# A graph layer on one core: degrees from first edges, degree products in four portions, statistics ahead of comparisons, wider scatter fills

## The chip, the cores and the metric

One Trainium2 chip, one of its cores. The metric is the device time of one execution in microseconds. The core's engines work side by side, each through its own queue in order: TensorE (PE in the profile, its weight loads apart as PEld), VectorE (DVE), ScalarE (ACT), GpSimd (POOL) and SyncE (SP), whose queue here only issues transfers. POOL also issues the indexed transfers (gathers and scatters).

## The reference

A layer norm in front, a message-passing layer over four relations, and a feed-forward block, on 625 nodes of 512 features and 20,625 edges sorted by destination (10,000 in both directions, and a loop per node). Cut to what matters:

```python
h = relu(layernorm(x))
for r in range(4):
    w_r = where(edge_type == r, edge_weight, 0)
    total_msg += (h[src] @ W_rel[r] + b_rel[r]) * w_r[:, None]
agg = segment_sum(total_msg, dst, 625)
deg = segment_sum(edge_weight, dst, 625)
agg = agg / maximum(deg, 1)[:, None]
hh = h @ W_self + b_self + agg
x1 = layernorm(h + hh) * ln1_g + ln1_b
ffn = gelu(x1 @ W_ffn1 + b_ffn1) @ W_ffn2 + b_ffn2
out = x + layernorm(x1 + ffn) * ln2_g + ln2_b
```

The change is about `deg`, the weighted degree of each node, and about the order of the work that stands beside it.

## The kernel before

Nodes lie in five blocks of 128 (`NB`), edges in 162 tiles of 128 (`NT`). The kernel first makes a **table** in device memory: for every relation and block, `table_rows` multiplies the transposed block `hT[i]` with the relation's weights (four pairs of matrix instructions, so eight by the profile's count), VectorE evicts the product (L358) and SP stores it. These are 20 steps, `step = r * NB + i`. In relation 0, `next_transposed` (L957) turns the next block in the middle of a step's products: `transposed` needs `z[:, i + 1]`, which `x_stats` (bn_stats, L335) and `pre_norm` (L325, and a root on POOL, L302) make on VectorE.

The first manual schedule (L937 to L998) writes down the order of TensorE, VectorE, ScalarE and POOL by hand: per engine, the instructions stand as the lines are called. A second one (L1273) emits a planned order for everything after the table; some of its first VectorE operations (L515, L525) appear in the trace among the last ones of the first schedule.

Besides the table, that first loop does four other jobs:

- **Block 0's sums.** Each edge of block 0's 31 columns of edges (`LN`) is compared with its 63 neighbours on either side (`line_sums`, L603 to L611, in `pieces` of four, eight, eight, eight and three columns, at the steps of `COLUMNS_AT`). POOL then scatters each column's weights into `cells` (`scatter`, L617), followed by a fill of the tile `idle` that only keeps POOL busy. At most `PACE * (step + 1)` scatters are issued up to a step. `load_sums` (L628) reads `cells` back as `sums_w`, which TensorE needs in the first product after the table (L1166).
- **Edge columns** at step 5: destination, relation and row numbers as columns (`outer_columns`, `edge_columns`, `degree_columns`, `group_columns`).
- **Degrees.** Node by node, a degree is a product of a 0/1 matrix with weights. `degree_hots` compares each tile's destinations with a window of 38 node rows (`W`), in bf16, 27 tiles to a chunk (`DG`). `degree_sums` multiplies, per tile, `w3` (the weight in three bf16 parts, and a 1) with that matrix into the two accumulators `pdeg`: three rows add up to the degree, the fourth counts edges per node. All six chunks are multiplied at step 13; `degree_end` and `spread_rows` bring the sums into columns, `rdeg` becomes the reciprocal.
- **First edges.** In the inner blocks three consecutive edges form a group (`EG`; 30 groups of tiles from tile 35 on, `GROUPS`, `GROUP0`): tile q of a group holds every group's edge q. Edges 1 and 2 of a group count for the group's sum only where they have the first one's destination (`wgt_g`). Where a node's edges begin inside a group, `first_edges` works out the group's number (`x_group`) from the counts, `load_first_edges` gathers it (`x_edges`), and `first_columns` (called by the later plan) makes columns and weights (`x_on`) of those edges.

`count_outside` counts edges outside their windows; were there any, a slow path would do all again.

Of the kernel before, what the change touches and what calls it, by code (L numbers as in the profile page):

```python
# [16 lines left out]
P = 128  # L17
# [120 lines left out]
def gnn_layer(ctx, tc, x, edges, edge_line, edge_groups, w_self, w_rel, w_ffn1, w_ffn2, rows_in, bf1_in, out, n_edges):  # L138
# [92 lines left out]
    load_x(3, 4)  # L231
    nc.sync.dma_start(cells[:P * NC * P, :].rearrange("(p c n) o -> p c (n o)", p=P, n=D // 2),
                      zeros.bitcast(F32).unsqueeze(1).to_broadcast([P, 2 * NC * P // D, D // 2]))
    load_x(4, NB)
# [35 lines left out]
    x_found = const.tile([P, 1], F32, name="x_found")  # L270
    wgt_g = const.tile([P, GROUPS, EG - 1], F32, name="wgt_g")
# [342 lines left out]
    idle = const.tile([P, PAUSE], BF16, name="idle")  # L614
# [25 lines left out]

    def degree_columns():
        nc.vector.tensor_sub(lim[:, 2, :], dst_f, starts.rearrange("p a b -> p (a b)")[:, :NT])
        nc.vector.tensor_sub(lim[:, 2, :], lim[:, 2, :], shift[:, 1, :])
        rel = early.tile([P, NT], BF16, name="rel")
        nc.vector.tensor_copy(rel, lim[:, 2, :])
        row_w = const.tile([P, W], BF16, name="row_w")
        nc.vector.tensor_copy(row_w, node_row[:, :W])
        w3 = const.tile([P, NT, 4], BF16, name="w3")
        nc.vector.memset(w3, 1.0)
        rest = lim[:, 3, :]  # L650
        nc.vector.tensor_copy(w3[:, :, 0], wgt)
        nc.vector.tensor_sub(rest, wgt, w3[:, :, 0])
        nc.vector.tensor_copy(w3[:, :, 1], rest)
        nc.vector.tensor_sub(w3[:, :, 2], rest, w3[:, :, 1])
        nc.vector.tensor_scalar(node_i[:, 1, :], node_i[:, 1, :], P - 1, None, op0=ALU.bitwise_and)
        nc.vector.tensor_copy(dst_mod, node_i[:, 1, :])
        return rel, row_w, w3
# [23 lines left out]
    def degree_sums(j0, nj, oc, w3):  # L681

        for j in range(j0, j0 + nj):
            s = ep.starts[j]
            lo, hi = max(s, 0), min(s + W, NP)
            for q in range(lo // D, (hi - 1) // D + 1):
                a, z_ = max(lo, q * D), min(hi, (q + 1) * D)
                if q not in pdeg:
                    pool, tag = (ps_add, "add") if q == 0 else (ps, "ps")
                    pdeg[q] = pool.tile([P, D], F32, tag=tag, name=f"pdeg_{q}")  # L690
                    nc.tensor.matmul(pdeg[q][:4, :], zeros[:, :4], zeros, start=True, stop=False)
                last = j == NT - 1 or ep.starts[j + 1] >= (q + 1) * D
                nc.tensor.matmul(pdeg[q][:4, a - q * D:z_ - q * D], w3[:, j, :], oc[:, j - j0, a - s:z_ - s],  # L693
                                 start=False, stop=last)
# [5 lines left out]
    def first_edges():  # L700
# [18 lines left out]
    def first_columns():  # L719
# [13 lines left out]
        nc.vector.tensor_mul(x_on, x_on, x_edges[:, :, 1:, 3].bitcast(F32))  # L733
        nc.vector.tensor_mul(x_on, x_on, rdeg[:, 1:NB - 1].unsqueeze(2).to_broadcast([P, INNER, EG - 1]))

    def degree_end():
# [5 lines left out]
        def spread_rows():  # L742
# [10 lines left out]
            nc.vector.tensor_scalar(rdeg, rdeg, 1.0, None, op0=ALU.max)  # L753
            nc.vector.reciprocal(rdeg, rdeg)
# [149 lines left out]
    DG = 27  # L904
# [22 lines left out]
    chunks = [(j0, min(DG, NT - j0)) for j0 in range(0, NT, DG)]  # L927
# [9 lines left out]
    with tc.manual_schedule(engines={PE, DVE, ACT, mybir.EngineType.Pool}):  # L937
# [6 lines left out]
        stats = x_stats(1)  # L944
        hots, made = [], 0
# [53 lines left out]
        assert not columns and not pieces and made == len(chunks) and len(scattered) == LN  # L999
# [405 lines left out]
```

## Time and profile before

| | us |
|---|---|
| median of three runs | 281.29 |
| the three runs | 282.1, 281.29, 280.1 |
| the profiled execution | 281.09 |
| its span, first to last instruction | 279.3 |
| busy: TensorE, VectorE, ScalarE, POOL | 253.7, 198.2, 82.1, 196.5 |
| first gather of table rows | 91.98 |

A timeline row reads: start and duration in us, engine, line, operation, what it writes and from what, shape, count of instructions merged, and in brackets the engine's idle time before it and what ended that. A row of the chain of waits has start, duration, engine and line. A row of stretches has the stretch, its length, busy time (and count) of PE, PEld, DVE, ACT and POOL, the granted TensorE clock as a share of full speed, the DMA engines' share, and GB/s. A row of groups has the total, the mean in ns, and the idle time before its instructions.

### The profile page before, as it was taken

What the parts mean: (1) busy time and instruction counts of PE and PEld (TensorE: products, weight loads), DVE (VectorE), ACT (ScalarE), POOL (GpSimd) and SP (SyncE); (2) the same over time, 40 slices, a digit from 0 to 9 for tenths busy, and PEclk for the clock granted to TensorE, in tenths of its full rate; (3) what the DMA queues carried; (4) which work ended last, traced back from release to release, by engine and by line L of the source; (5) the groups of instructions that cost most, each with busy time, mean ns of one, the idle gap of its engine ahead of it and who ended that gap; (6) DMA issues with size and microseconds to landing.
All of it is one profiled execution on the core that took longest, in us unless ns stands there. A gap on an engine that the chain in (4) does not pass through costs nothing.

```text
span 279.3 us, 3679 instructions
## 1 busy us (share of the span) xinstructions
PE 253.7 (91%) x1081; PEld 141.5 (51%) x1081; DVE 198.2 (71%) x469; ACT 82.1 (29%) x190; POOL 196.5 (70%) x378
## 2 busy tenths in 40 slices
PE   8897999999999998876798969999999999998990
PEld 3433444465544443533354424459476783853960
DVE  4985799983559641898978768658669986856514
ACT  3110030000000385683946022224234252430320
POOL 6788998997030788887887878888889888831000
PEclk9999999999999999999689999999999999999997
DMA  7999899631722888988665796766666668640001
GB/s 218 380 424 394 229 372 346 217 116 38 263 80 89 299 257 282 332 263 313 181 185 169 253 323 213 235 188 188 189 186 182 186 171 255 190 133 13 38 2 39
DMA packets 25127, 58.86 MB, mean 211 GB/s; under 512 B 3937, under 2 KB 6241, under 8 KB 24850
## 3 DMA queue, kind: packets, MB, share of 16 engines
q0 software_dynamic: 9488, 27.57, 32.9%
q1 hardware_dynamic: 15328, 29.60, 29.9%
q10 hardware_dynamic: 290, 1.44, 1.5%
q8 instruction: 9, 0.15, 0.2%
q14 instruction: 12, 0.10, 0.1%
HBM read 50.75 MB, written 7.85 MB: 210 GB/s over the span
## 4 chain that ended last, share of the span: by engine, by line
PE 47%; DVE 16%; POOL 16%; DMA 11%; issue 7%; ACT 1%; DVEq 0%; SPq 0%; POOLq 0%
PE pt L351 19%; POOL ms L1033 11%; DMA ms<-table,row_i 9%; PE pu L830 7%; PE po L848 5%; PE acc L1166 4%; PE acc L1083 4%; POOL zeros L1036 3%; PE pz L371 3%; DVE ea L1061 2%; PE pdeg L693 2%; DMA xs<-in_x_dram 1%; DVE od L525 1%; PE bank L548 1%; DVE es L1061 1%
## 5 line engine op out<-in xcount | busy, mean ns | idle before, releaser
L1033 POOL DMA_INDIRECT ms<-table,row_i x99 | 98.3, 993 | 32.0 <-DVE x_cols L724 12.3
L351 PE MATMUL pt<-wr,hT 128*128 128x512 f32 x160 | 70.4, 595 | 0.2 <-DMA wr<-in_L_gnn_W_rel_dram 0.2
L351 PEld LDWEIGHTS pt<-wr,hT 128*128 128x128 f32 x160 | 29.8, 190 | 35.0 <-issue 34.6
L617 POOL DMA_INDIRECT cells<-weight,cell x31 | 37.1, 1197 | 6.1 <-issue 5.0
L1061 DVE SCALAR_TENSOR_TENSOR ea<-ms,wgt_g,ea 128x512 f32<-128x512 f32 x40 | 30.0, 750 | 15.2 <-DMA ms<-table,row_i 13.3
L830 PEld LDWEIGHTS pu<-x1T,w_sb 128*128 128x128 f32 x320 | 37.5, 192 | 5.7 <-issue 3.8
L533 ACT ACTIVATE ohw<-os,w 128x128 fp32r<-128x128 f32 x64 | 20.1, 389 | 63.8 <-DVE os L515 63.6
L830 PE MATMUL pu<-x1T,w_sb 128*128 128x128 f32 (+1 forms) x320 | 38.0, 275 | 0.9 <-ACT x1T L1215 0.9
L1043 ACT ACTIVATE ea<-ms,ed 128x512 f32<-128x512 f32 x30 | 20.7, 691 | 59.6 <-DMA ms<-table,row_i 46.6
L848 PE MATMUL po<-w_sb,gT 128*128 128x512 f32 (+3 forms) x96 | 36.0, 522 | 0.0
L1083 PE MATMUL acc<-es,oh 128*128 128x512 f32 x58 | 30.7, 619 | 1.8 <-DVE rs_z L766 0.9
L1036 POOL MEMSET zeros<- 128x200 bf16 x99 | 28.8, 290 | 0.0
L1166 PE MATMUL acc<-tr,sums_w 128*128 128x512 f32 x60 | 27.5, 592 | 0.0
L358 DVE SCALAR_TENSOR_TENSOR m<-pt,rx,brel_bc 128x512 f32<-128x512 f32 x20 | 14.8, 745 | 13.8 <-PE pt L351 13.8
L848 PEld LDWEIGHTS po<-w_sb,gT 128*128 128x128 f32 (+1 forms) x96 | 16.6, 188 | 14.8 <-issue 12.3
L548 PE MATMUL bank<-od,ohw 128*128 128x500 f32 (+16 forms) x64 | 17.1, 393 | 4.9 <-ACT ohw L533 4.1
L371 PE MATMUL pz<-ws_sb,hT 128*128 128x512 f32 x40 | 19.6, 612 | 0.8 <-DVE n_out L419 0.8
L1061 DVE SCALAR_TENSOR_TENSOR es<-ms,wgt_g,ea 128x512 f32<-128x512 f32 x20 | 14.8, 742 | 6.8 <-DMA ms<-table,row_i 6.6
L834 ACT ACTIVATE gT<-pu,bf 128x128 f32<-128x128 f32 (+1 forms) x40 | 13.7, 364 | 16.5 <-PE pu L830 16.4
L548 PEld LDWEIGHTS bank<-od,ohw 128*128 128x128 f32 x64 | 11.2, 202 | 12.5 <-ACT ohw L533 6.7
L1166 PEld LDWEIGHTS acc<-tr,sums_w 128*128 128x128 f32 x60 | 11.2, 190 | 12.4 <-issue 12.4
L1083 PEld LDWEIGHTS acc<-es,oh 128*128 128x128 f32 x58 | 10.3, 194 | 12.7 <-issue 5.3
(191 smaller groups left out, 289.4 us busy)
## 6 DMA issues: line engine op xcount, KB each, us to landing
tr<-table SPq DMA_DIRECT2D x14, 512.0 KB, 5.8
table<-m SPq DMA_DIRECT2D x20, 256.0 KB, 2.2
w_sb<-in_L_gnn_W_ffn_dram SPq DMA_DIRECT2D x2, 2048.0 KB, 12.7
wr<-in_L_gnn_W_rel_dram SPq DMA_DIRECT2D x3, 1024.0 KB, 8.1
ms<-table,row_i POOLq DMA_INDIRECT x99, 3.7
rows<-in_rows_dram SPq DMA_DIRECT2D x1, 1536.0 KB, 13.0
cells<-zeros SPq DMA_DIRECT2D x1, 1280.0 KB, 9.5
sums_w<-cells ACTq DMA_DIRECT2D x1, 1280.0 KB, 6.4
```

The costliest lines, as they stand in the source:

```text
L351: nc.tensor.matmul(p, hT[i][:, k, :], wr_sb[r][:, k, :], start=(k == 0), stop=(k == KD - 1))
L371: nc.tensor.matmul(p[0], hT[i][:, k, :], ws_sb[:, k, :], start=(k == 0), stop=(k == KD - 1))
L548: nc.tensor.matmul(bank[b, n0][:, (lo - n0) * NC:(end - n0) * NC], box["ohw"][:, k - k0, part, :], box[k][:, :(end - lo) * NC], start=star ...
L617: i = nc.gpsimd.indirect_dma_start(out=cells[:, :], out_offset=bass.IndirectOffsetOnAxis(ap=cell[:, k:k + 1], axis=0), in_=weight[:, k:k + ...
L830: nc.tensor.matmul(pu[:, :nn], w1_sb[:, k, f * P:(f + 1) * P], x1T_b()[:, k, :nn], start=(k == 0), stop=(k == KD - 1))
L848: nc.tensor.matmul(po[h][:n, :w], box["gT"][:, f, at], w2_sb[:, f, c], start=(f == 0), stop=(f == KF - 1))
L1033: nc.gpsimd.indirect_dma_start(out=ms[j], out_offset=None, in_=table[:, :], in_offset=bass.IndirectOffsetOnAxis(ap=row_i[:, j:j + 1], axis=0))
L1036: nc.gpsimd.memset(zeros[:, :PAUSE], 0.0)
L1043: nc.scalar.activation(box["sum"], ms[j], AF.Copy, scale=wgt[:, j:j + 1])
L1061: nc.vector.scalar_tensor_tensor(to, ms[j], wgt_g[:, k, q - 1:q], box["sum"], op0=ALU.mult, op1=ALU.add)
L1083: nc.tensor.matmul(acc[bs], ohs[0][:, q, :].bitcast(F32), box["sum"], start=(k == 0), stop=last)
L1166: nc.tensor.matmul(acc[b,], sums_w[b][:, c, :], kept[(b, c) if (b, c) in kept else c], start=first, stop=last)
```

## The change

Degrees: of each group of three tiles only the first stays in the degree product, with the weight of the whole group as far as the destinations agree (`wgt_g` summed, plus the first's weight). The 1 that counts stands only at first edges of groups, so the counts give the group's number without a division. What a node has in the group where it begins inside is added later, in `first_columns`, where clamp and reciprocal of `rdeg` now stand too. 102 tiles are left (`ND`), in four chunks of up to 26.

Order: a chunk is compared at steps 7, 8, 10 and 11 (`HOTS_AT`) and multiplied right after the next step's table products; the degrees' later steps come one step earlier. Group and degree columns move from step 5 to step 6, group first. `x_stats` and `pre_norm` of block `step + 3` stand ahead of the comparisons of edge columns, which move to steps 0, 2, 4, 9 and 12. Block 1's `pre_norm` is called ahead of `set_limits` (72 small fills on POOL). The count of outside edges comes one step earlier, `load_sums` one step later. Blocks 3 and 4 of x are loaded in one transfer ahead of the zero fill of `cells`. The fill after a scatter has 400 elements in place of 200, and the pace is 3.

```diff
-    load_x(3, 4)
+    load_x(3, NB)
     nc.sync.dma_start(cells[:P * NC * P, :].rearrange("(p c n) o -> p c (n o)", p=P, n=D // 2),
                       zeros.bitcast(F32).unsqueeze(1).to_broadcast([P, 2 * NC * P // D, D // 2]))
-    load_x(4, NB)
...
-    idle = const.tile([P, PAUSE], BF16, name="idle")
+    idle = const.tile([P, 2 * PAUSE], BF16, name="idle")
...
+    deg_tiles = [*range(GROUP0), *range(GROUP0, GROUP0 + EG * GROUPS, EG), *range(GROUP0 + EG * GROUPS, NT)]
+    ND = len(deg_tiles)
+    deg_at = [(slice(0, GROUP0), slice(0, GROUP0)), (slice(GROUP0, GROUP0 + GROUPS), None),
+              (slice(GROUP0 + GROUPS, ND), slice(GROUP0 + EG * GROUPS, NT))]
...
-        rel = early.tile([P, NT], BF16, name="rel")
-        nc.vector.tensor_copy(rel, lim[:, 2, :])
+        rel = early.tile([P, ND], BF16, name="rel")
...
-        w3 = const.tile([P, NT, 4], BF16, name="w3")
-        nc.vector.memset(w3, 1.0)
-        rest = lim[:, 3, :]
-        nc.vector.tensor_copy(w3[:, :, 0], wgt)
-        nc.vector.tensor_sub(rest, wgt, w3[:, :, 0])
+        w3 = const.tile([P, ND, 4], BF16, name="w3")
+        nc.vector.memset(w3, 0.0)
+        nc.vector.memset(w3[:, deg_at[1][0], 3], 1.0)
+        whole, rest = early.tile([P, ND], F32, name="deg_w"), lim[:, 3, :ND]
+        for to, of in deg_at:
+            if of is None:
+                nc.vector.tensor_copy(rel[:, to], grouped(lim[:, 2, :])[:, :, 0])
+                nc.vector.reduce_sum(whole[:, to], wgt_g, axis=mybir.AxisListType.X)
+                nc.vector.tensor_add(whole[:, to], whole[:, to], grouped(wgt)[:, :, 0])
+            else:
+                nc.vector.tensor_copy(rel[:, to], lim[:, 2, of])
+                nc.vector.tensor_copy(whole[:, to], wgt[:, of])
+        nc.vector.tensor_copy(w3[:, :, 0], whole)
+        nc.vector.tensor_sub(rest, whole, w3[:, :, 0])
...
-                    pool, tag = (ps_add, "add") if q == 0 else (ps, "ps")
-                    pdeg[q] = pool.tile([P, D], F32, tag=tag, name=f"pdeg_{q}")
+                    pdeg[q] = ps_add.tile([P, D], F32, tag="add", name=f"pdeg_{q}")
...
-        near = 1.5 * 2.0 ** 23
-        g = xw[:, 1, :]
-        nc.vector.tensor_scalar(g, first[:, :INNER], -(GROUP0 * P + (EG - 1) / 2), 1.0 / EG, op0=ALU.add, op1=ALU.mult)
-        nc.vector.tensor_scalar(g, g, near, None, op0=ALU.add)
-        nc.vector.tensor_scalar(g, g, -near, 0.0, op0=ALU.add, op1=ALU.max)
-        nc.vector.tensor_scalar(x_group, g, float(GROUPS * P), None, op0=ALU.min)
+        nc.vector.tensor_scalar(x_group, first[:, :INNER], -1.0, 0.0, op0=ALU.add, op1=ALU.max)
...
+        nc.vector.reduce_sum(x_deg, x_on, axis=mybir.AxisListType.X)
+        nc.vector.tensor_add(rdeg[:, 1:NB - 1], rdeg[:, 1:NB - 1], x_deg)
+        nc.vector.tensor_scalar(rdeg, rdeg, 1.0, None, op0=ALU.max)
+        nc.vector.reciprocal(rdeg, rdeg)
         nc.vector.tensor_mul(x_on, x_on, rdeg[:, 1:NB - 1].unsqueeze(2).to_broadcast([P, INNER, EG - 1]))
...
-    DG = 27
+    DG = 26
-    PACE = 2
+    PACE = 3
-    COLUMNS_AT = 0, 1, 4, 7, 10
-    COLUMNS_OF_EDGES_AT, LOAD_AT = 5, 16
-    DEGREES_AT, SPREAD_AT, FIRST_AT = 13, 14, 15
+    COLUMNS_AT, HOTS_AT = (0, 2, 4, 9, 12), (7, 8, 10, 11)
+    COLUMNS_OF_EDGES_AT, LOAD_AT = 5, 17
+    DEGREES_AT, SPREAD_AT, FIRST_AT = 12, 13, 14
...
-        stats = x_stats(1)
+        pre_norm(1, x_stats(1))
...
-        pre_norm(1, stats)
         line_columns()
-        stats = x_stats(2)
+        pre_norm(2, x_stats(2))
...
                     transposed(hT[i + 1], z[:, i + 1, :], f"h{i + 1}")
-                    if i + 2 < NB:
-                        pre_norm(i + 2, stats)
 
                 table_rows(r, i, next_transposed if r == 0 and i + 1 < NB else None)
+                while hots:
+                    degree_sums(*hots.pop(0))
+                if step + 3 < NB:
+                    pre_norm(step + 3, x_stats(step + 3))
                 if step in COLUMNS_AT:
                     next_columns()
-                if step + 3 < NB:
-                    stats = x_stats(step + 3)
...
                     edge_columns()
+                if step == COLUMNS_OF_EDGES_AT + 1:
+                    group_columns()
                     cols = degree_columns()
-                    group_columns()
-                if step > COLUMNS_OF_EDGES_AT and made < len(chunks):
-                    hots.append(degree_hots(*chunks[made], *cols))
-                    made += 1
+                if step in HOTS_AT:
+                    hots.append(degree_hots(*chunks[HOTS_AT.index(step)], *cols))
...
                 if step == DEGREES_AT:
-                    for made_ in hots:
-                        degree_sums(*made_)
                     spread_rows = degree_end()
...
-                if step == R * NB - 2:
+                if step == R * NB - 3:
                     total_outside = count_outside()
```

More of the change, by code (lines that the diff above doesn't have):

```diff
@@ L270, in gnn_layer @@
     x_found = const.tile([P, 1], F32, name="x_found")
+    x_deg = const.tile([P, INNER], F32, name="x_deg")
     wgt_g = const.tile([P, GROUPS, EG - 1], F32, name="wgt_g")
@@ L683, in degree_sums @@
         for j in range(j0, j0 + nj):
-            s = ep.starts[j]
+            s = ep.starts[deg_tiles[j]]
             lo, hi = max(s, 0), min(s + W, NP)
@@ L688, in degree_sums @@
                 if q not in pdeg:
-                    pool, tag = (ps_add, "add") if q == 0 else (ps, "ps")
-                    pdeg[q] = pool.tile([P, D], F32, tag=tag, name=f"pdeg_{q}")
+                    pdeg[q] = ps_add.tile([P, D], F32, tag="add", name=f"pdeg_{q}")
                     nc.tensor.matmul(pdeg[q][:4, :], zeros[:, :4], zeros, start=True, stop=False)
-                last = j == NT - 1 or ep.starts[j + 1] >= (q + 1) * D
+                last = j == ND - 1 or ep.starts[deg_tiles[j + 1]] >= (q + 1) * D
                 nc.tensor.matmul(pdeg[q][:4, a - q * D:z_ - q * D], w3[:, j, :], oc[:, j - j0, a - s:z_ - s],
@@ L752, in spread_rows @@
             nc.vector.reduce_sum(rdeg, sums[:, :, 0:3], axis=mybir.AxisListType.X)
-            nc.vector.tensor_scalar(rdeg, rdeg, 1.0, None, op0=ALU.max)
-            nc.vector.reciprocal(rdeg, rdeg)
         return spread_rows
@@ L921, in gnn_layer @@
     CH = 2
-    PACE = 2
+    PACE = 3
     FIRST_PIECE = 4
-    COLUMNS_AT = 0, 1, 4, 7, 10
-    COLUMNS_OF_EDGES_AT, LOAD_AT = 5, 16
-    DEGREES_AT, SPREAD_AT, FIRST_AT = 13, 14, 15
-    chunks = [(j0, min(DG, NT - j0)) for j0 in range(0, NT, DG)]
+    COLUMNS_AT, HOTS_AT = (0, 2, 4, 9, 12), (7, 8, 10, 11)
+    COLUMNS_OF_EDGES_AT, LOAD_AT = 5, 17
+    DEGREES_AT, SPREAD_AT, FIRST_AT = 12, 13, 14
+    chunks = [(j0, min(DG, ND - j0)) for j0 in range(0, ND, DG)]
     later_groups = [(a, min(2, NE - a)) for a in range(0, NE, 2)]
@@ L943, in gnn_layer @@
         pre_norm(0, x_stats(0))
-        stats = x_stats(1)
-        hots, made = [], 0
+        pre_norm(1, x_stats(1))
+        hots = []
         for k, n in ((0, 1), (1, 1), (2, 2)):
@@ L995, in gnn_layer @@
                     load_first_edges()
-                if step == R * NB - 2:
+                if step == R * NB - 3:
                     total_outside = count_outside()
             later_loads(r)
-        assert not columns and not pieces and made == len(chunks) and len(scattered) == LN
+        assert not columns and not pieces and len(HOTS_AT) == len(chunks) and len(scattered) == LN
     early_stack.close()
```

## The prediction

> **What bounds the kernel now.** I read the slices of the span and the chain of waits first, then the timeline of each engine up to 110 us, because every edit lies before the first gather of table rows.
>
> ```profile
> PEclk9999999999999999999689999999999999999997
> PE 47%; DVE 16%; POOL 16%; DMA 11%; issue 7%; ACT 1%; DVEq 0%; SPq 0%; POOLq 0%
> 23.91 36.05 PE pt L351 x84
> 60.26 3.23 PE pdeg L693 x128
> 63.71 1.10 PE pdeg L693 x44
> 91.98 0.95 POOL L1033 DMA_INDIRECT ms<-table,row_i  x1 [12.29 <-DVE x_cols L724]
> ```
>
> TensorE holds the largest share of the chain, at full clock but for one dip in the middle and the end. From 23.91 it runs 84 table products without a gap, 36.05/84 = 0.429 us each, then all the degree products, then the rest of the table. The gathers on POOL start at 91.98, after the last block of the table. What follows is one planned order that the change leaves alone, so what TensorE gains or loses before that moves the end by about as much. I therefore make the sum on TensorE's queue up to the end of the table. Only the first blocks show it waiting:
>
> ```profile
> 8.56 0.63 PE L309 MATMUL tp_h<-ident,z 128*128 128x128 f32 x4 [1.06 <-DVE rx L326]
> 9.39 3.67 PE L351 MATMUL pt<-wr,hT 128*128 128x512 f32 x8 [0.19 <-DMA wr<-in_L_gnn_W_rel_dram]
> 13.33 3.60 PE L351 MATMUL pt<-wr,hT 128*128 128x512 f32 x8
> 17.43 0.66 PE L309 MATMUL tp_h<-ident,z 128*128 128x128 f32 x4 [0.50 <-DVE rx L326]
> 17.92 3.60 PE L351 MATMUL pt<-wr,hT 128*128 128x512 f32 x8
> 23.25 0.66 PE L309 MATMUL tp_h<-ident,z 128*128 128x128 f32 x4 [1.73 <-DVE rx L326]
> ```
>
> **The change part by part: statistics ahead of comparisons.** The third row's eight products last 8 x 0.429 = 3.43 us, so TensorE could have gone on at 16.76; it went on at 17.43. After the fifth it could have at 21.35, and did at 23.25. The loss is 0.67 + 1.90 = 2.57 us, caused by VectorE doing comparisons of edges ahead of the next block's normalisation.
>
> ```profile
> 6.29 2.12 DVE L325 TENSOR_SCALAR z<-xs,mv_x 128x512 f32<-128x512 f32 x1
> 15.95 0.68 DVE L335 BATCH_NORM_STATS2 st_x<-xs 128x6 f32<-128x512 f32 x1
> 17.36 0.74 DVE L358 SCALAR_TENSOR_TENSOR m<-pt,rx,brel_bc 128x512 f32<-128x512 f32 x1
> 5.48 2.66 POOL L398 MEMSET lim<- 128x35 f32 x72
> ```
>
> Statistics and normalisation of a block take 17.36 - 15.95 = 1.41 us. Put ahead of the comparisons, block 3 is ready before 15.95, where its statistics begin now, and is wanted at 16.76. Block 4 follows the next table eviction (17.36 at the earliest under today's comparisons of four columns): 17.36 + 0.7 + 1.41 = 19.5, wanted at 16.76 + 0.44 + 3.43 = 20.6. I take the whole 2.57 us. Blocks 3 and 4 now come in one transfer ahead of the zero fill; should it land late, nothing is gained, which is the other bound.
>
> Block 1's normalisation took 2.12 us beside the 72 POOL fills; POOL's root for block 1 now stands ahead of those fills, so it runs free of them. That is worth nothing: behind its transposes TensorE waited 0.19 us for the weights' transfer anyway. The fills move some 2 us later, and with them `place`, on which the first scatter hangs.
>
> **Degrees from first edges.** 172 products become 112 (60 of 162 edge tiles fall away; the ten that straddle node row 512 keep two). At 3.23/128 = 0.025 us that is 1.5 us. Four portions in place of one cost three more changes between table and degree products, which no row shows: between 0 and 0.2 us each; I take 0.1, near the gapless changes of the chain above. Gain 1.2 us.
>
> **The count of outside edges** goes one block earlier:
>
> ```profile
> 83.70 0.75 DVE L358 SCALAR_TENSOR_TENSOR m<-pt,rx,brel_bc 128x512 f32<-128x512 f32 x1 [1.42 <-PE pt L351]
> 86.66 0.83 DVE L411 TENSOR_REDUCE cnt<-lim 128x1 f32<-128x648 f32 x1
> 87.40 0.74 DVE L358 SCALAR_TENSOR_TENSOR m<-pt,rx,brel_bc 128x512 f32<-128x512 f32 x1
> ```
>
> The last eviction could start at 83.70 + 3.43 = 87.13 and started at 87.40 behind it: 0.3 us gained. One block earlier the 1.42 us of idle time before an eviction covers the count.
>
> **The new wait.** In the old order all degree products stood at step 13, long after their comparisons. Now portion 0 is compared at step 7 and multiplied right behind step 8's table products. Behind it on TensorE's queue stand all later table products, and behind these the stores and gathers. VectorE lags there:
>
> ```profile
> 29.15 0.75 DVE L358 SCALAR_TENSOR_TENSOR m<-pt,rx,brel_bc 128x512 f32<-128x512 f32 x1 [2.67 <-PE pt L351]
> 44.53 1.22 DVE L675 TENSOR_TENSOR oc<-rel,row_w 128x1026 bf16<-128x1026 bf16 x1
> 45.67 0.74 DVE L358 SCALAR_TENSOR_TENSOR m<-pt,rx,brel_bc 128x512 f32<-128x512 f32 x1
> 46.33 1.20 DVE L603 TENSOR_TENSOR same<-line_key 128x1016 f32<-128x1016 f32 x1
> 39.66 0.60 DVE L649 MEMSET w<- 128x648 bf16 x1
> 70.04 0.19 DVE L754 RECIPROCAL rdeg<-rdeg 128x5 f32<-128x5 f32 x1
> ```
>
> Step 4's eviction starts at 29.15, having waited for TensorE. From there VectorE is busy without a gap until the first comparison ends at 45.67: 16.5 us. The changed order holds the same work (eviction 4, comparisons of eight edge columns, eviction 5, edge, group and degree columns, eviction 6, comparison), and eviction 7 besides, 46.33 - 45.67 = 0.66. The degree columns get some seven small operations more (0.1 to 0.2 each by the last row) and fill 408 elements where L649 fills 648, with the other weight operations a third narrower: 0.3 more, between -0.5 and 0.9. So portion 0 is ready 17.5 us after step 4's eviction starts. TensorE, whose step 4 ends at 23.91 + 12 x 0.429 = 29.06, needs 32 x 0.429 = 13.7 us for steps 5 to 8 and asks at 42.8 on the old clock, when VectorE is at 29.15 + 17.5 = 46.6. **A wait of 3.8 us appears**, whatever the front gains, since both sides move with step 4. Bounds 2.5 (the small operations favourable, the later-phase comparisons that VectorE slips in here, L515 and L525, placed elsewhere) to 4.7. The next portions find VectorE caught up: one table step is 3.43 us, an eviction with a comparison 1.8.
>
> What does such a gap do to TensorE's clock? One gap of this kind is in the trace, and the kernel's end is another:
>
> ```profile
> 132.87 1.25 PE L548 MATMUL bank<-od,ohw 128*128 128x260 f32 x4 [2.98 <-ACT ohw L533]
> 130.00:135.00 5.00, 1.73 (x6) 1.12 (x7) 5.00 (x14) 3.19 (x10) 4.37 (x7) 1.00 0.65 190
> 135.00:137.00 2.00, 0.58 (x3) 0.17 (x2) 2.00 (x6) 2.00 (x7) 1.83 (x4) 0.55 0.66 207
> 140.00:142.00 2.00, 2.00 (x7) 1.40 (x6) 1.74 (x5) 1.46 (x6) 1.72 (x3) 0.50 0.61 166
> 142.00:147.00 5.00, 5.00 (x16) 2.38 (x15) 3.58 (x9) 1.90 (x4) 4.46 (x8) 1.00 0.64 194
> 275.00:276.00 1.00, 0.00 (x0) 0.00 (x0) 0.80 (x2) 0.00 (x0) 0.00 (x0) 0.57 0.00 0
> ```
>
> The sixth value behind the stretch's length is the granted clock. After the gap of 2.98 us and five thin microseconds it stood at about half from 135.2 to 142.0, 6.8 us. The waits of 0.50 and 1.73 us earlier left it whole. A gap of 3.8 us is longer than all of these. If half clock follows, table products there cost double: over 6.8 us that would lose 3.4; if the clock holds, 0. I take the middle, 1.7 us. The Trainium skill ("TensorE: Matmul & The Clock Gate", Part 1) has a rule that speaks against this change: after an idle window of about 3.4 us, free-running, the array falls to half clock until a busy window has passed. One such window at half would be an estimated 1.7 us, by that page; the two windows' worth of low clock in the rows above agrees with its length (6.8), not with a single window.
>
> **The scatters.** Each of the 31 gets a fill twice as wide, and pace 3 lets them be issued earlier than POOL can take them.
>
> ```profile
> L617 POOL DMA_INDIRECT cells<-weight,cell x31 | 37.1, 1197 | 6.1 <-issue 5.0
> 17.63 0.28 POOL L620 MEMSET idle<- 128x200 bf16 x1
> 3.06 0.10 POOL L283 MEMSET xw<- 128x15 f32 x1
> 67.53 0.96 POOL L617 DMA_INDIRECT cells<-weight,cell  x1 [0.17 <-issue]
> 69.99 0.33 ACTq L628 DMA_DIRECT2D sums_w<-cells  x1
> sums_w<-cells ACTq DMA_DIRECT2D x1, 1280.0 KB, 6.4
> 86.94 3.60 PE L1166 MATMUL acc<-m,sums_w 128*128 128x512 f32 x8
> ```
>
> From 15 to 200 elements a fill grows by 0.18 us, so 200 more cost about 0.2 (bounds 0.18, and 0.28 for plain doubling). POOL's queue is nearly gapless here, so 30 x 0.2 = 6 us, and an estimated 1.2 us for the later start (of the 2 us by which the fills move, a part stands beside VectorE's own wait for `place`); the last scatter ends near 75.7 instead of 68.5, the load of `sums_w` goes out 1.5 us later and lands at 75.7 + 1.5 + 6.4 = 83.6. TensorE asks for it at 86.94 today. The three `x_edges` loads queue behind the scatters and finish near 80, with use after 88. Cover enough: 0 us. Four small operations move into `first_columns`, 0.2 us each, after the step that the first gather is put down to: 0.
>
> **Sum**, against the profiled execution's own 281.09 us (span 279.3 and 1.8 around it): -2.57 - 1.2 - 0.3 + 3.8 + 1.7 = +1.4. That gives 282.5; the median of the three runs is 0.2 above the profiled one and they spread over 2.0, so I forecast **282.6 us**.
>
> **The rivals.** *The clock holds* (0.22): the same wait without half clock, -0.3, 280.8 us. For it: in the gap of 2.98 us the clock was still whole for more than 2 us after work resumed. Against: the gap is longer here. *No wait* (0.18): VectorE is earlier than I count, or TensorE's order is not the written one. Then -4.1: 277.0 us. For it: VectorE's L515 and L525 rows among the degree columns, 2 us of work for a later phase, show that written orders are interleaved. Against: without a gap in VectorE's timeline from 29.15 to 45.67, only removed work can help, and none is removed ahead of portion 0. *The front waits stay* (0.04), the one transfer of blocks 3 and 4 landing late, so the reordering does not do what it says: 282.5 + 2.6 = 285.1 us.
>
> *Slower, by the scatters* (0.08):
>
> ```profile
> 41.37 0.71 POOL L620 MEMSET idle<- 128x200 bf16 x1
> 90.00:125.00 35.00, 31.74 (x92) 15.60 (x90) 22.08 (x58) 22.54 (x58) 29.31 (x45) 1.00 0.85 281
> ```
>
> One fill took 0.71 us beside VectorE's casts, so a wide fill can cost far more than 0.2. `sums_w` lands at 77.6 + 30c with c the extra cost of a fill. TensorE would ask at 86.94 + 1.4 = 88.3, so c over 0.36 makes it wait; at c = 0.55 by 5.8 us. TensorE idles 3.3 us between 90 and 125 and can win that back: +2.5 on the forecast, 285.1 us.
>
> **How the numbers follow.** The forecast has 0.48; its own range, from its bounds on the wait and the clock, is 280.7 to 284.4. For 8 in 10 I reach from 276.8, which takes in most of the no-wait case, to 285.0. About 1% (2.8 us, so 278.5 and 284.1 about the median) is what can be told from no change. Faster: the no-wait case, nearly all of its 0.18: 0.17. Slower: the two slow rivals but for their low ends, 0.10, and the upper tail of the forecast, 0.06: 0.16. The same: 0.67.
>
> **What would show it.** A degree row on TensorE near 40 us whose idle time is put down to the comparison `oc`, some 3.8 us, with the clock below 1.00 in the following stretch; no wait over 0.2 us at the transposes of blocks 3 and 4; 112 degree products in four groups; fills near 0.48 us and the last scatter near 75; first gather near 93. A gapless TensorE from 12 to 80 us would prove the central step wrong; `acc` waiting for `sums_w`, the scatters' step.

## The result, and the profile after

| | before | after |
|---|---|---|
| median | 280.88 us (four runs, 280.1 to 282.1) | 284.94 us (four runs, 284.19 to 285.25) |
| profiled execution, its span | 281.09, 279.3 | 284.65, 282.8 |
| TensorE goes on past the front (chain of waits) | 23.91 | 21.62 |
| last block of the table ends, `acc` starts | 86.94 | 90.54 |
| first gather of table rows | 91.98 | 95.49 |
| from the table's end to the span's end | 192.4 | 192.3 |

The ratio is 1.0136, with a 95% interval of [1.0091, 1.0182]: slower by 1.4%. The span grew by 3.5 us, the table's end came 3.6 us later and the rest kept its length, so everything is decided before 91 us. First two lines of the page of the changed kernel: the granted clock in 40 slices, and the engines' shares of the chain of waits.

```profile
PEclk9999997999999999999579999999999999999998
POOL 28%; PE 26%; DMA 18%; DVE 15%; issue 9%; ACT 2%; SPq 1%; POOLq 0%; DVEq 0%; ACTq 0%
```

The clock has a new 7 in the seventh slice (42 to 49 us). TensorE's share of the chain fell from 47 to 26%, but not because of the table, whose products hold 18% of the chain (19% before): behind the table, the chain now follows the gathers (`ms` on POOL, 20% in place of 11%). The loss is in the seventh slice, and TensorE's timeline in the changed kernel shows the place:

```profile
13.24 0.63 PE L309 MATMUL tp_h<-ident,z 128*128 128x128 f32 x4 [0.86 <-DVE rx L326]
...
17.14 0.60 PE L309 MATMUL tp_h<-ident,z 128*128 128x128 f32 x4
...
21.02 0.60 PE L309 MATMUL tp_h<-ident,z 128*128 128x128 f32 x4
21.45 19.05 PE L351 MATMUL pt<-wr,hT 128*128 128x512 f32 x44
...
45.79 0.98 PE L706 MATMUL pdeg<-oc,w 128*4 128x21 bf16 x26 [4.98 <-DVE oc L689]
46.70 4.95 PE L351 MATMUL pt<-wr,hT 128*128 128x512 f32 x8
51.58 0.81 PE L706 MATMUL pdeg<-oc,w 128*4 128x38 bf16 x26
52.32 7.13 PE L351 MATMUL pt<-wr,hT 128*128 128x512 f32 x16
...
60.59 3.70 PE L351 MATMUL pt<-wr,hT 128*128 128x512 f32 x8
...
90.54 3.60 PE L1173 MATMUL acc<-m,sums_w 128*128 128x512 f32 x8
```

In the chain of waits of the changed kernel the run behind them reads:

```profile
21.62 5.17 PE pt L351 x12
```

That is 2.29 us ahead of the old 23.91. The transposes of blocks 3 and 4 (17.14, 21.02) wait for nothing any more; those of block 2 now do, 0.86 us. After 44 gapless table products comes the new wait: portion 0 stands 4.98 us for its comparison `oc`. The step behind it takes 4.95 us where a step between two portions takes 3.70 (row at 60.59). The windows of the changed kernel (granted clock: sixth value behind the length) say why:

```profile
45.00:46.00 1.00, 0.21 (x8) 0.21 (x8) 1.00 (x2) 0.00 (x0) 0.84 (x2) 0.92 1.03 382
46.00:47.00 1.00, 1.00 (x25) 0.93 (x22) 1.00 (x2) 0.00 (x0) 1.00 (x2) 0.50 0.68 254
...
49.00:50.00 1.00, 1.00 (x3) 0.38 (x2) 0.00 (x0) 0.00 (x0) 1.00 (x2) 0.88 0.04 10
50.00:51.00 1.00, 1.00 (x3) 0.38 (x2) 0.00 (x0) 0.00 (x0) 0.83 (x2) 1.00 0.02 1
```

A mean of 0.92 is 0.16 us at half clock, one of 0.88 is 0.24; with the three whole microseconds between, that is 3.4 us at half, from 45.84 to 49.24. VectorE's timeline in the changed kernel, on the way to that comparison:

```profile
26.86 0.75 DVE L358 SCALAR_TENSOR_TENSOR m<-pt,rx,brel_bc 128x512 f32<-128x512 f32 x1 [0.23 <-PE pt L351]
...
34.03 0.72 DVE L456 TENSOR_SCALAR key<-lim 128x32 f32<-128x32 f32 x1
...
37.22 0.89 DVE L525 TENSOR_SCALAR od<-key_row,key 128x440 fp32r<-128x440 f32 x1
...
44.57 1.17 DVE L689 TENSOR_TENSOR oc<-rel,row_w 128x988 bf16<-128x988 bf16 x1
```

From the eviction of step 4 (26.86) to the end of the first comparison (45.74) VectorE takes 18.88 us, with hardly a gap. Before the change the same way took 16.5 without the eviction of step 7. Two short operations in it last 0.72 and 0.89 us; the experiments below show them at half that.

The front, last: rows of VectorE and POOL from the timelines of the changed kernel.

```profile
7.22 2.94 DVE L569 CAST line_f<-line 128x474 f32<-128x474 int32 x1 [0.56 <-DMA line<-in_edge_line_dram]
...
7.25 2.65 POOL L398 MEMSET lim<- 128x35 f32 x72
```

A cast that took 0.39 us in the kernel before lasts until the 72 fills of POOL that start beside it have ended. Block 2's statistics stand behind it; that is the 0.86 us above.

### The profile page after: what moved, and what is told of

Read it like the earlier page. It is cut to its first block, busy times and chain, and to the rows that moved or that the text cites. A ratio compares the mean times of both kernels' runs of the same rounds, so it can differ in the third digit from the quotient of the medians.

```text
span 282.8 us, 3559 instructions
## 1 busy us (share of the span) xinstructions
PE 255.3 (90%) x1021; PEld 141.7 (50%) x1021; DVE 198.6 (70%) x473; ACT 81.4 (29%) x190; POOL 198.1 (70%) x378
## 4 chain that ended last, share of the span: by engine, by line
POOL 28%; PE 26%; DMA 18%; DVE 15%; issue 9%; ACT 2%; SPq 1%; POOLq 0%; DVEq 0%; ACTq 0%
POOL ms L1040 20%; PE pt L351 18%; DMA ms<-table,row_i 15%; POOL zeros L1043 6%; PE pu L840 3%; PE po L858 2%; DMA line<-in_edge_line_dram 2%; POOL ms_first L1097 2%; DMA ms_first<-table,x_row 1%; PE pdeg L706 1%; DVE od L525 1%; DVE line_f L569 1%; ACT ea L1050 1%; DVE ea L1068 1%; DVE m L358 1%
## 5 line engine op out<-in xcount | busy, mean ns | idle before, releaser
L351 PE MATMUL pt<-wr,hT 128*128 128x512 f32 x160 | 72.5, 605 | 0.9 <-DMA wr<-in_L_gnn_W_rel_dram 0.9
L617 POOL DMA_INDIRECT cells<-weight,cell x31 | 32.7, 1054 | 8.5 <-issue 4.8
L548 PE MATMUL bank<-od,ohw 128*128 128x500 f32 (+16 forms) x64 | 18.0, 413 | 4.3 <-ACT ohw L533 3.7
L548 PEld LDWEIGHTS bank<-od,ohw 128*128 128x128 f32 x64 | 11.9, 212 | 11.4 <-ACT ohw L533 6.4
```

The lines of the kernel that those rows point to most:

```text
L351: nc.tensor.matmul(p, hT[i][:, k, :], wr_sb[r][:, k, :], start=(k == 0), stop=(k == KD - 1))
L548: nc.tensor.matmul(bank[b, n0][:, (lo - n0) * NC:(end - n0) * NC], box["ohw"][:, k - k0, part, :], box[k][:, :(end - lo) * NC], start=star ...
L617: i = nc.gpsimd.indirect_dma_start(out=cells[:, :], out_offset=bass.IndirectOffsetOnAxis(ap=cell[:, k:k + 1], axis=0), in_=weight[:, k:k + ...
```

## The experiments

Lines in the diffs have hardly any context. Kernels of one group shared a chip with the kernel before, whose time is given with them.

**Both kernels again** (unedited), on one chip with the next two; before in that group: 281.43 us.

> The changed kernel once more, unedited, because the chip of the first four runs gave the kernel before 297.6 us in place of 280.9, so that they can't be set against the first result. Expected by the theory of the wait: the wait of 5 us and the half clock behind it are there as before, whatever the chip. If the ratio to the kernel before is again 1.01, the chip only scales; if it is below 1, the chip charges the kernel before for something that the change removes, and the table of the kernel before should end later than 86.9 us.

> The kernel before, unedited, for its profile on this chip. Rival to 'the chip only scales': in the run with the wide fill alone, TensorE stood idle for short pieces inside the run of degree products, put down to issue, and its clock halved after them; if that is so here too, the 172 products last 7 us in place of 4.9 and step 14's products 5 us or more in place of 3.7, and the fill had no part in it. If the products last 4.9 us, the fill did it.

The changed kernel took 286.01 us, ratio 1.0153 [1.0117, 1.0188]; the kernel before 282.48, ratio 1.0019 [0.9981, 1.0056]. This was another chip than the one with 297.6 us, and the kernel before takes on it what it took at first: the first result is confirmed, and the question about that chip stays open. TensorE's timeline of the changed kernel, and windows, in this repeat:

```profile
22.21 19.05 PE L351 MATMUL pt<-wr,hT 128*128 128x512 f32 x44
...
46.55 0.98 PE L706 MATMUL pdeg<-oc,w 128*4 128x21 bf16 x26 [4.97 <-DVE oc L689]
47.45 5.96 PE L351 MATMUL pt<-wr,hT 128*128 128x512 f32 x8
...
92.31 3.60 PE L1173 MATMUL acc<-m,sums_w 128*128 128x512 f32 x8
```

```profile
45.00:46.00 1.00, 0.00 (x0) 0.00 (x0) 1.00 (x2) 0.00 (x0) 0.87 (x2) 0.61 1.07 408
...
51.00:52.00 1.00, 1.00 (x3) 0.45 (x2) 0.00 (x0) 0.00 (x0) 0.83 (x2) 0.50 0.02 1
```

The wait is the same to 0.01 us, but here half clock lasts from 45.22 (0.61 is 0.78 us at half) to 52.0, 6.8 us: two stretches of 3.4 instead of one. The slow step takes 5.96.

For the kernel before, the same view, which serves as the measure for what follows:

```profile
24.15 36.22 PE L351 MATMUL pt<-wr,hT 128*128 128x512 f32 x84
60.30 0.38 PE L691 MATMUL pdeg<-zeros 128*4 128x512 bf16 x1
...
65.15 3.70 PE L351 MATMUL pt<-wr,hT 128*128 128x512 f32 x8
...
87.35 3.60 PE L1166 MATMUL acc<-m,sums_w 128*128 128x512 f32 x8
```

From the start of the gapless run to the table's end it takes 87.35 - 24.15 = 63.20 us. The same difference in the changed kernel is 90.54 - 21.45 = 69.09, and 70.10 in the repeat.

**The front alone**: the kernel before with statistics and normalisation ahead of the comparisons, and blocks 3 and 4 in one transfer.

```diff
-    load_x(3, 4)
+    load_x(3, NB)
...
-    load_x(4, NB)
...
-        stats = x_stats(1)
+        pre_norm(1, x_stats(1))
...
+                if step + 3 < NB:
+                    pre_norm(step + 3, x_stats(step + 3))
                 if step in COLUMNS_AT:
```

> The kernel before with the statistics ahead of the comparisons alone (blocks 3 and 4 of x in one transfer; order of comparisons, degrees, fills as before). Theory: the front gains 2.3 us by itself, as in the change (the steady run of table products starts at 21.4 in place of 23.7), the table ends 2.3 us earlier than in the kernel before, and the time falls by about 2.3 us (0.8%). Rival: the gain is given back after the table, and the time stays within 0.5 us of the kernel before.

278.81 us, ratio 0.9913 [0.9882, 0.9945]. TensorE's timeline of that kernel:

```profile
21.07 36.22 PE L350 MATMUL pt<-wr,hT 128*128 128x512 f32 x84
...
84.27 3.60 PE L1162 MATMUL acc<-m,sums_w 128*128 128x512 f32 x8
```

The run starts 3.08 us earlier than in the row at 24.15, and the table ends 3.08 earlier: 84.27 - 21.07 = 63.20 again. A gain in the front goes through to the table's end undiminished. The time fell by 2.6 us against the group's 281.43, where the interval allows 1.5 to 3.3.

**Products late, narrow fills, later limits**: the changed kernel with three edits.

```diff
-    idle = const.tile([P, 2 * PAUSE], BF16, name="idle")
+    idle = const.tile([P, PAUSE], BF16, name="idle")
...
-        set_limits(0)
-        set_limits(1)
         line_columns()
         pre_norm(2, x_stats(2))
+        set_limits(0)
+        set_limits(1)
...
-                while hots:
+                while hots and step == DEGREES_AT:
```

> The changed kernel with all degree portions behind step 12's table products, the old fill of 200, and the 72 small fills moved behind POOL's work on the edge line. Theory: the cast that lasted 2.94 us beside those fills lasts 0.4, the wait of 0.86 us before block 2's transposes is gone, the wait on the comparison too, and the table ends 0.9 us earlier than with the portions late alone (near 84.1 in place of 85.1). Against the changed kernel on the same chip 6 to 8 us less. Rival: the later small fills now stand before the first scatters and hold VectorE's casts elsewhere, and the table ends no earlier than 85.

277.24 us, ratio 0.9811 [0.9766, 0.9856]: faster than both kernels. Its TensorE timeline:

```profile
20.76 0.66 PE L309 MATMUL tp_h<-ident,z 128*128 128x128 f32 x4 [0.69 <-DVE rx L326]
21.25 32.78 PE L351 MATMUL pt<-wr,hT 128*128 128x512 f32 x76
53.96 0.38 PE L704 MATMUL pdeg<-zeros 128*4 128x512 bf16 x1
...
57.31 3.70 PE L351 MATMUL pt<-wr,hT 128*128 128x512 f32 x8
...
82.94 3.60 PE L1173 MATMUL acc<-m,sums_w 128*128 128x512 f32 x8
```

No gap at 40 us, and 82.94 - 21.25 = 61.69 us. Against 63.20 the difference is the grouping alone: 112 products in one run (53.96 to 57.31, 3.35 us) for 172 (60.30 to 65.15, 4.85), **1.5 us gained**. Against the changed kernel's 69.09 it is the portions: **7.4 us lost**, 4.98 of them the wait. The later limits moved the cost of the 72 fills rather than removed it: `line_f`'s cast takes 0.41 us here, and a normalisation at 12.97 takes 2.95 instead, which leaves block 3 a wait of 0.24 us and block 4 the 0.69 in the first row.

**The products late, alone**, on two other chips; before there: 297.56 and 296.69 us.

```diff
-                while hots:
+                while hots and step == DEGREES_AT:
```

> The changed kernel with all four degree portions multiplied behind step 12's table products; comparisons, fills and everything else as in the change. Theory (the wait of the first portion is what the change loses): the wait of 4.98 us on the comparison is gone, TensorE runs from 21 to 54 us without a gap at full clock, the table ends 6 to 7 us earlier than in the changed kernel (first product after the table near 84 in place of 90.54), and the time is 278 us, under the kernel before. Rival (the loss lies after the table, in the later loads and the longer first columns): the time stays within 1.5 us of the changed kernel's 284.9.

> The late products alone, on another chip than the first time: all four portions are multiplied after step 12, as before the change. Theory (the early wait and the half clock that follows it are the loss): no gap in the run of step products, TensorE's table ends 7 us earlier than in the changed kernel (about 85), time 278 to 279.5, ratio to before 0.985 to 0.995. Rival (the gain of the first time, 0.969, belonged to that chip, and the loss is in the scatters' longer fills or in the columns): table end at 88 or later, time 281 or more, ratio 1.00 or above.

287.32 us, ratio 0.969 [0.963, 0.975], and 285.15 us, ratio 0.9593 [0.9528, 0.9657]. Both times miss what I expected (278, and 278 to 279.5), since both chips were ones on which the kernel before takes 16 us longer (below), and so do the times of all runs on these chips that follow. The timeline of TensorE doesn't miss it in the second run:

```profile
21.17 32.78 PE L351 MATMUL pt<-wr,hT 128*128 128x512 f32 x76
53.88 0.38 PE L704 MATMUL pdeg<-zeros 128*4 128x512 bf16 x1
...
57.50 3.70 PE L351 MATMUL pt<-wr,hT 128*128 128x512 f32 x8
...
83.13 3.60 PE L1173 MATMUL acc<-m,sums_w 128*128 128x512 f32 x8
```

The gap at 40 us is gone and the table ends at 83.13 (85.06 the first time), 7.4 us ahead of the changed kernel, with wide fills and early limits as in it. From the run's start it is 83.13 - 21.17 = 61.96 us, near the 61.69 with the other edits. So the portions carry the loss, whatever the other edits do.

**Narrow fills alone**, on the same two chips:

```diff
-    idle = const.tile([P, 2 * PAUSE], BF16, name="idle")
+    idle = const.tile([P, PAUSE], BF16, name="idle")
```

> The changed kernel with the old fill of 200 elements. Theory A (the wide fills held VectorE's casts up, so that the wait came out at 5.0 in place of 3.8): VectorE's stretch from step 4's eviction to the end of the first comparison falls from 18.8 us to about 17.6, the wait on the comparison to about 3.8, and the time by about 1.2 us to 283.7. Theory B (the degree columns' added small operations cost more than the 0.3 us I gave them): the stretch stays above 18.4, the wait above 4.6, and the time within 0.4 us of 284.9. Half clock follows the wait in both.

> The changed kernel with the fill behind each scatter narrow again, nothing else. Theory (the wide fills stretch VectorE's casts, and with them the wait of portion 0): VectorE from the eviction of step 4 to the end of the first comparison about 17.4 us (18.8 in the changed kernel), wait of portion 0 3.5 to 3.9 us (5.0), half clock as before, time 1.0 to 1.5 us under the changed kernel, about 283.5 to 284.5, ratio to before 1.008 to 1.012. Rival (the casts are slow for another reason): wait 4.9 to 5.2, time 285 to 286, ratio 1.014 or more.

293.09 us, ratio 0.9892 [0.9837, 0.9947]; 289.85 us, ratio 0.9769 [0.971, 0.9829]. Second run, timelines of TensorE and of VectorE:

```profile
44.37 0.81 PE L706 MATMUL pdeg<-oc,w 128*4 128x21 bf16 x26 [3.44 <-DVE oc L689]
45.11 5.40 PE L351 MATMUL pt<-wr,hT 128*128 128x512 f32 x8
...
89.40 3.60 PE L1173 MATMUL acc<-m,sums_w 128*128 128x512 f32 x8
```

```profile
26.98 0.75 DVE L358 SCALAR_TENSOR_TENSOR m<-pt,rx,brel_bc 128x512 f32<-128x512 f32 x1 [0.31 <-PE pt L351]
...
34.04 0.37 DVE L456 TENSOR_SCALAR key<-lim 128x32 f32<-128x32 f32 x1
...
36.72 0.45 DVE L525 TENSOR_SCALAR od<-key_row,key 128x440 fp32r<-128x440 f32 x1
...
43.14 1.18 DVE L689 TENSOR_TENSOR oc<-rel,row_w 128x988 bf16<-128x988 bf16 x1
```

VectorE's stretch is 43.14 + 1.18 - 26.98 = 17.34 us instead of 18.88, and the wait 3.44 (3.53 in the first run) instead of 4.98. The wide fill lengthens the stretch and the wait by 1.5 us, and two rows show half of it: `key` 0.37 instead of 0.72, `od` 0.45 instead of 0.89. Most of the rest lies in casts (L450 0.38 instead of 0.54, L458 0.20 instead of 0.36, L659 0.41 instead of 0.71). Comparisons of two tensors keep their length (L603 is 1.21 us with either fill). What this is worth in time no two runs on one chip show. The Trainium skill ("SBUF — State Buffer", "Who interferes with whom") has it that casts, copies and scalar operations of VectorE can take a pair of ports that GpSimd needs, that whichever came first blocks the other for its whole length, and that an operation on two tensors does not contend with a GpSimd operation that only writes. The kinds of operation that grew here agree with that, but for a reduction (L660, 0.63 instead of 0.32), which starts while a stretched cast still runs.

**Wide fills in the kernel before**, on the first of those chips:

```diff
-    idle = const.tile([P, PAUSE], BF16, name="idle")
+    idle = const.tile([P, 2 * PAUSE], BF16, name="idle")
```

> The kernel before with the fill of 400 elements alone. Theory A of the fills: VectorE's stretch from step 4's eviction to the end of the first comparison grows from 16.5 us to about 17.5, which nobody waits for in this order; scatters end near 74 in place of 68.5, and the time stays within 0.5 us of 280.9. Theory B: the stretch stays at 16.5 within 0.3.

297.19 us against 297.56, ratio 0.9988 [0.9952, 1.0024]. Its profiled execution took 301.38 us, so only VectorE's rows are read from it. VectorE's stretch grows there too, from 16.5 to 17.8 us (31.59 to 49.41), but in that order nobody waits at its end. `key` takes 0.72 us there too. In the old order the wide fill costs nothing that the times can tell (at most 0.7 us by the interval); in the new one it makes the wait 1.5 us longer.

**TensorE kept busy through the wait**, on the two chips: 22 products of zeros, which nothing reads, ahead of portion 0.

```diff
+                if step == HOTS_AT[0] + 1:
+                    for _ in range(22):
+                        nc.tensor.matmul(warm, zeros[:, :P], zeros, start=True, stop=True)
                 while hots:
```

> The changed kernel with 22 products of zeros (128x512, bf16, some 0.21 us each, 4.7 in all) put between step 8's table products and the first degree portion; their results are not used. Theory (half clock after the wait is a cost of its own): the granted clock stays 1.00 from 45 to 50 us, step 9's products last 3.4 us in place of 4.9, the time falls by 1.5 us to 283.4 though nothing waits less. Rival (the clock is not tied to the gap): half clock comes all the same, and the time stays at 284.9 or rises by what the added products overrun.

> The changed kernel with 22 products of zeros ahead of portion 0, in the time in which TensorE waits for the first comparison. Theory (TensorE's idling costs one stretch at half clock): clock 1.00 from 40 to 50 us, the step product behind it 3.7 us (5.0 in the changed kernel), table end 1.3 to 1.7 us earlier, time 283.5 to 284.5. Rival (the slow step has another reason, operands that come late or contention): step product still 4.9 to 5.0 us, time 285 to 286.

292.61 us, ratio 0.9854 [0.98, 0.9908]; 291.43 us, ratio 0.9818 [0.9768, 0.9869]. Second run, TensorE's timeline:

```profile
40.34 4.91 PE L972 MATMUL warm<-zeros 128*128 128x512 bf16 x22
...
45.80 0.81 PE L706 MATMUL pdeg<-oc,w 128*4 128x21 bf16 x26 [0.24 <-DVE oc L689]
46.54 3.70 PE L351 MATMUL pt<-wr,hT 128*128 128x512 f32 x8
...
89.14 3.60 PE L1176 MATMUL acc<-m,sums_w 128*128 128x512 f32 x8
```

One of its windows, to be set beside the same microsecond of the changed kernel above:

```profile
46.00:47.00 1.00, 1.00 (x25) 0.79 (x22) 1.00 (x2) 0.00 (x0) 1.00 (x2) 1.00 0.53 195
```

Portion 0 starts at the same moment as in the changed kernel (45.79), but the clock is 1.00 in every microsecond from 40 to 54, in the first run too; the step behind it takes 3.70 us, and the table ends 1.4 us earlier. So the slow step was the clock, and the clock fell because TensorE idled. The times don't separate these kernels from those with narrow fills (the order differs between the chips), and the changed kernel itself did not run there.

**Grouped degrees in the kernel before**, on the second of those chips. The degree columns, `x_group`, `first_columns` and `DG` are those of the change; order, fills and statistics those of before (only the group columns stand ahead of the degree columns).

```diff
-        rel = early.tile([P, NT], BF16, name="rel")
-        nc.vector.tensor_copy(rel, lim[:, 2, :])
+        rel = early.tile([P, ND], BF16, name="rel")
...
+        nc.vector.tensor_add(rdeg[:, 1:NB - 1], rdeg[:, 1:NB - 1], x_deg)
...
-    DG = 27
+    DG = 26
...
-    chunks = [(j0, min(DG, NT - j0)) for j0 in range(0, NT, DG)]
+    chunks = [(j0, min(DG, ND - j0)) for j0 in range(0, ND, DG)]
```

> The kernel before with the degrees computed the new way (one column for each group's first edge and those of the other edges' weights, 26 to 28 products a portion of step), but all multiplied after step 12 and with statistics, transfers and fills as before. Theory (a degree product is 0.025 to 0.03 us, and fewer of them save their own time): the run of degree products takes 3.3 to 3.6 us (4.85 before), table end 1.2 to 1.5 us earlier, time about 279.5 to 280.2 where the kernel before has 281.4, ratio 0.993 to 0.997. Rival (the added small operations of VectorE and POOL in the first columns come late and give it back): table end within 0.3 us of before, ratio 0.999 to 1.002.

294.41 us, ratio 0.9948 [0.9895, 1.0001]: inconclusive in time. The ratio lies where I expected it, but not for the reason given, as TensorE's timeline shows:

```profile
60.56 1.30 PE L707 MATMUL pdeg<-oc,w 128*4 128x21 bf16 x45
62.17 0.25 PE L707 MATMUL pdeg<-oc,w 128*4 128x38 bf16 x4 [0.32 <-issue]
...
69.62 5.44 PE L352 MATMUL pt<-wr,hT 128*128 128x512 f32 x8
```

After 45 products the run breaks into groups of about five with 0.3 to 0.5 us between, in which TensorE waits for nothing that the profile shows. 112 products take 9.3 us instead of 3.35, and half clock follows. The fills are narrow here, so such pieces come without the wide fill too, against what was thought possible for the repeat of the kernel before. What the grouping is worth is therefore read from the group on the other chip (1.5 us), not from here.

## Why the prediction was partly right

The time lies in the range (276.8 to 285.0), 0.06 us below its upper edge. That is luck: two of the four runs lie above it, and so does the median of the repeat (286.01). The forecast's own range, 280.7 to 284.4, is exceeded; its bounds on the wait and the clock, added up, reach from 279.6 to 285.2. The forecast of 282.6, no change that can be told, was 2.3 us too low, and the case "slower by over 1%", given 0.16, is where the median came out, with an interval that reaches down to 1.0091. The mechanism forecast happened: a wait of portion 0 for its comparison, followed by half clock. What failed are sizes, and of the terms that missed, only the half clock came out cheaper than forecast. TensorE's sum closes on the rows above: front -2.29, grouping -1.51, wait +4.98, half clock +1.42, three more switches +1.00, together +3.60; the table's end moved by 90.54 - 86.94 = 3.60.

- **The new wait, 3.8, was 4.98.** The working behind it held: with narrow fills VectorE's stretch was 17.34 us where I had 17.5, and the wait 3.44 (TensorE asks some 0.3 us later than I counted, behind a product of zeros that opens `pdeg`). What it left out was the step on **the scatters**, costed at 0 because their last user has cover. The cover was there (`acc` at 90.54 waits for nothing, a fill takes 0.45 us, forecast 0.48), but I looked only at what the fills do to POOL's queue. I had quoted a fill stretched by VectorE's casts, and not asked for the reverse: the fills stretch the casts, by 1.5 us, on the one path that TensorE waits for.
- **Degrees, -1.2.** 60 products less are 1.51 us, as worked out. Each of the three more switches costs 0.33 us where I took 0.1 with a bound of 0.2: a run of eight table products between two switches takes 3.63 us, 0.2 over 8 x 0.429, a cost that stands outside the portions' own rows. Net -0.5.
- **Half clock, 1.7, was 1.42** (step 9: 51.58 - 46.70 = 4.88 for 3.63; portion 0: 0.98 for 0.81), and 2.44 in the repeat. Bounds of 0 to 3.4 held both; that the middle came so near is luck. The run with zero products shows the cause. With narrow fills, second run, the low stretch lay wholly in table products and cost 5.33 - 3.63 = 1.70 us, half its length; here a part of it fell on portion 0, which lost only 0.17. By the Trainium skill ("TensorE: Matmul & The Clock Gate", Part 1) half clock comes in windows of about 3.4 us that run free; the 3.4 and 6.8 us here agree, and the estimate of 1.7 us by one window is what the 1.70 shows.
- **The front, -2.57, was -2.29.** Blocks 3 and 4 wait no more, as forecast. That moving block 1's normalisation ahead of the 72 fills was "worth nothing" was wrong: the weights landed earlier this time and block 1's products started 0.68 us earlier (8.71, 9.39 before), but the fills then fell on the line columns' cast, block 2 waited 0.86 us, and its transposes started 0.35 us later than before (13.24, 12.89). The front alone, in the kernel before, gave 3.08; 0.41 of it comes from the repeat of the kernel before, whose run starts at 24.15, against 23.74 in its first profile.
- **The count, -0.3**: the table's last eviction starts 0.20 us behind `acc`, 0.46 before (87.40 - 86.94), so the eviction gains what I said. The first gather doesn't show it: it follows the table's end by 4.95 us, 5.04 before, and by 5.42 and 5.14 in the repeats.
- **The rivals.** "The clock holds" and "no wait" fell with the rows at 45.79 and 46.70; "the front waits stay" with those at 17.14 and 21.02; "slower by the scatters" fell in its mechanism, since nothing waits for `sums_w`, though its first sentence (a fill beside VectorE's casts costs far more than alone) was the lead to the term I missed.

In one sentence: the portions cost TensorE 7.4 us (about 6 with narrow fills: 89.40 - 21.57 - 61.69 = 6.14), and the front and the grouping, which won 3.8, could not pay for them. Not tried were the later limits alone, and narrow fills or late products alone on the chip of the 277.24 us.

## What to carry to other kernels

Moving small products closer to their operands only helps if the engine that makes the operands is ahead: compare the two queues from their last common point, and ask what runs on other engines beside that work. A filler on an idle engine is not free when another engine's casts take longer beside it (1.5 us in all here) and stand on the path that is waited for. The four waits of 3.44 to 4.98 us for portion 0 cost 1.2 to 2.4 us at half clock besides their own length. How short a wait may be without that is not shown: half clock also followed the gap of 2.98 us with thin microseconds around it, in the kernel before, and the many gaps of 0.3 to 0.5 us in the grouped kernel. Where a wait can't be removed, products that nothing reads bridge it, as in the run with products of zeros.

## What was not expected of the hardware

- **Chips differ, and the verdict with them.** The kernel before took 281.43 us (17 runs) on one chip, and 297.56 and 296.69 on two others. Each chip was measured in one session only, so the chip and the session can't be told apart. From the table's end to the span's end seven kernels took 197 to 201 us on those two (an eighth, in the execution of 301.38 us, 204), while the six with times of 277 to 286 us, the changed kernel and the one before among them, took 192 to 193.5. Besides, long runs of small products break up as in the rows at 62.17: the grouped kernel loses 69.36 - 61.69 = 7.7 us there. Portions of 26 products never broke up. The edits of the changed kernel that keep its portions (narrow fills, TensorE kept busy) came out at 0.977 to 0.989 of before on those chips, so the change itself may well be faster there than the kernel before; that was argued from them, not run. What causes the breaks stays open: late products broke up in one run (5.0 us for 112) and hardly in the other (3.6).
- **Half clock comes in one stretch or two for the same wait.** With waits of 4.98 and 4.97 us it lasted 3.4 and 6.8. In the first, products resumed at 45.79, as the clock fell (45.84); in the second it fell at 45.22, 1.3 us before they resumed at 46.55. With narrow fills it fell 0.3 us before they resumed (45.08 and 45.41, first run) and 1.5 us after (45.86 and 44.37, second run), and lasted 3.4 both times. That a stretch must be busy nearly from its start to be the last is a reading of these four, not a test.
- **Mostly, one operation of VectorE beside the 72 fills lasts until they have ended**: `line_f`'s cast 2.94 us in the changed kernel, the next operation 2.82 in its repeat, a normalisation 2.95 with the limits later; the fills take 2.65. Not always: in the second run with the products late the cast (0.41 us) and the next operation (0.33) kept their length, the fills took 2.90, and block 2 did not wait. What decides it stays open.
